# A transformer block on one core: one of the four W2 weight pieces of the second QKV stage is prepared in the last attention unit of the first row

## The chip, the core and the metric

The kernel runs on one NeuronCore of a Trainium2 chip. Five engines of that core appear in this text: PE (TensorE, matrix products; its weight loads are listed apart as PEld), DVE (VectorE), ACT (ScalarE), POOL (GpSimd) and SP (SyncE, which here only issues DMAs; its queue is listed as SPq). The metric is the device time of one execution in microseconds (us).

## What is computed

One transformer block with modulation by a condition, in f32, for x of shape (2, 2048, 512): two batch rows of 2048 tokens. There are 16 heads of 32 columns; the MLP is 2048 wide.

```python
mod = silu(condition) @ Wada + bada
sh_a, sc_a, gt_a, sh_m, sc_m, gt_m = split(mod, 6, axis=1)
xm = layernorm(x, g1, be1) * (1 + sc_a) + sh_a
q, k, v = heads(xm @ Wqkv)
attn = softmax(causal(q @ k.T * 32 ** -0.5))
x = x + gt_a * ((attn @ v) @ Wproj + bproj)
xm = layernorm(x, g2, be2) * (1 + sc_m) + sh_m
x = x + gt_m * (gelu(xm @ W1 + b1) @ W2 + b2)
```

## The kernel before

The two batch rows go through the first half of the block one after the other, each as a `Row` object, and the MLP then takes both at once. The stages, by the trace's time from the start of the span:

- QKV of row 0, to about 167 us: layernorm statistics on DVE, scaling of x on ACT, transposes and products on PE. The products use the Strassen-Winograd form: a 2 x 2 block product with seven multiplications in place of eight, which needs sums of blocks on both sides.
- Attention of row 0 (`attention_phase`, L619), to about 715. Its 16 units are the pairs of a group c of four heads and a block i of 512 queries. The last group takes its query blocks in the order 0, 2, 1, 3, so the last unit is group 3, block 3, with 15 steps. A step is one tile of 128 keys (two where they are cut by the causal edge) for the four heads: PE makes the scores `st`, ACT the exponentials `e` (L670), POOL zeroes what lies behind the diagonal (L682, an affine_select), PE multiplies by the values `vv`, and the exponentials of a unit are summed into a chain `ee` (`add`, L693), which PE then sums over the keys with a matrix of ones (`sm`). The sums of exponentials run on POOL as one operation over four heads; in the last unit alone they run on DVE, as four operations, one a head (L698). Beside that PE and DVE already work out the row maxima of the unit to come (`s`, `mx`).
- Projection of row 0 and the statistics of the second layernorm (`project_phase`, L1295), to about 777.
- QKV of row 1, the second QKV stage, to about 950; attention of row 1, to about 1463; its projection, to about 1525; the MLP of both rows, to the end.

The last unit also prepares the projection behind it (`prepare`, L448): at its steps 5 to 9 DVE copies and multiplies the gate into Wproj (L456, L457, L461), at steps 11 to 14 POOL adds a bias to four tiles of x (L467, tiles named kst because they lie in old key room) and DVE multiplies outputs by reciprocal sums (L469). In the projection POOL adds the bias to the next tiles (L1338) and multiplies later outputs by reciprocals (L1351).

The MLP, too, uses the Strassen-Winograd form, and its weights are put into that form ahead of time, in twelve "pieces" made by the class `Pieces` (L1205): eight of W1 in the first QKV stage (f = 0 to 7) and four of W2 in the second (f = 8 to 11). A W2 piece has seven blocks of 128 x 896 f32, and each block is itself seven sub-blocks of 128 columns. `load` puts eight DMAs of 128 KB into SP's queue (L1239). `add` queues the sums, all on POOL (L1251): four over whole blocks (512 wide) for the outer form, then four for each of the tiles that hold the blocks, over the sub-blocks of the inner form. `store` writes the seven blocks to the scratch array w2d with DMAs that POOL issues (L1271). `plan(f, room, load, start)` says at which tick the piece is loaded and from which its sums are queued; `tick` issues one queued operation, or two where more than 12 are waiting. The blocks lie in room that is not in use just then: spare key and query tiles and the part of the value tile `vv` that row 1 hasn't reached. In the second QKV stage, one tick goes with each step of PE's products:

```python
for f, (room, load, start) in enumerate((
    (room_2, 0, 6), (room_1, 16, 24), (room_2, 47, 56), (room_3, 74, 80),
), FC // 2):
    pieces.plan(f, room, load, start)
```

Each engine takes its instructions in the order in which the program issues them; every DMA of SP and POOL stands in the queue of the engine that issues it, and what waits holds up all behind it. So the order of work around the change follows from where in the program a tick, a load of x (L919) or a `prepare` step stands. PE's order comes from the same program text, with due times for the scores of later units (`due`).

The names to follow are these: kst and qst are key and query tiles (and whatever is kept in their room), vv the values, e the exponentials, ee their sum, x, k, lo the rows and stored keys of the QKV stage, ps_xt the transposes of x.

Of the kernel before, what the change touches and what calls it, by code (L numbers as in the profile page):

```python
# [8 lines left out]
F32 = mybir.dt.float32  # L9
# [8 lines left out]
P = 128  # L18
# [9 lines left out]
def dit_block_kernel(  # L28
# [36 lines left out]
    nc = tc.nc  # L65
# [3 lines left out]
    FC = HID // P  # L69
    NT = T // P  # L70
# [13 lines left out]
    def pool(name, bufs=1, **kw):  # L84
        return tc.tile_pool(name=name, bufs=bufs, reuse_waits="tile", **kw)
# [31 lines left out]
    for n in range(2):  # L117

        f = bp.tile([P, QB + P], BF16, tag=f"fold{n}", name=f"fold{n}")
# [10 lines left out]
    def picks():  # L130
# [61 lines left out]
    w2d = [  # L192
        dram.tile([P, C, 7, P], F32, tag=f"w2d{n}", name=f"w2d{n}")
        for n in range(7)
    ]
# [12 lines left out]
    def act(ins):  # L208

        return tc.keep_in_program_order(ins)  # L210
# [84 lines left out]
    class Row:  # L295


        def __init__(self, b):
            self.b = b
            self.vv = bp.tile([P, NT, D], F32, tag="vv", name="vv")  # L300
            self.kst, self.qst, self.pools = {}, {}, {0: bp}
            self.at = 0
            self.todo = [
                item for u, (_, i) in enumerate(units) for item in self.banks_of(u, i)
            ]
            self.mx = None
            self.unsplit, self.paced = [], False
            self.spent = 0
            self.rows_made = 0

        def banks_of(self, u, i):

            for h in range(HC):
                for t in range(TQ):
                    for kb in range(i):
                        yield u, kb, [(h, t)]
                    if t == 1 and h % 2:
                        yield u, i, [(h - 1, t), (h, t)]
                    elif t == 2:
                        yield u, i, [(h, 0), (h, t)]  # L320
                    elif t == 3:
                        yield u, i, [(h, t)]
# [296 lines left out]
    def attention_phase(row):  # L619
        b, vv, kst, qst = row.b, row.vv, row.kst, row.qst  # L620
        row.paced = True
        with pool(f"att{b}") as ap, pool(
            f"ps_st{b}", bufs=HC, space=PSUM
        ) as ps_stp, pool(f"ps_o{b}", space=PSUM) as ps_op:
            row.pools[1] = ap

            n_bank = [0]

# [71 lines left out]
            def add_to(u, chain, es):  # L700
                add(u, chain, chain, es)
# [44 lines left out]
            def flush(upto):  # L746
                while pending and pending[0][0] <= upto:
                    pending.pop(0)[1]()
# [25 lines left out]
            for u, (c, i) in enumerate(units):  # L774
# [5 lines left out]
                for n_step, tiles in enumerate(steps_of[u]):  # L780
                    last = n_step == steps - 1
                    if n_step == 0:
# [5 lines left out]
                    n = row.count(  # L788
                        due(u, starts[u] + n_step) - QB // 2,
                        u + AHEAD - (n_step < 2 and u > 0),  # L790
                    )
                    if u == 0 and n_step < LAG:

                        n = max(n, HC)
# [9 lines left out]
                    row.inverses(u, n_step)  # L804
                    if u == len(units) - 1:
                        row.prepare(n_step)
                    if make_rows and not last:
                        row.rows(u + 1)
                    flush(now)
# [30 lines left out]
                    if n_step < i * TQ:  # L840
                        k = n_step % TQ
# [36 lines left out]
                    pending.sort(key=lambda p: p[0])  # L878
                    now += 1
            flush(now + LAG)  # L880

    w1_v = W1.rearrange("(c p) f -> p c f", p=P)
    w2_v = W2.rearrange("(c p) f -> p c f", p=P)
# [2 lines left out]
    S1, S2, A11, S4, A12, A22, S3 = range(7)  # L886
# [11 lines left out]
    class Qkv:  # L898
# [239 lines left out]
        def run(self, hp, also, early=()):  # L1138
# [63 lines left out]
                step()  # L1202
            assert not self.loads

    class Pieces:  # L1205


# [17 lines left out]
        def load(self, f, room):  # L1225
            parts = self.blocks(f, room)
            for n, i, k in BASE:
                if f < FC // 2:
                    at = (f + i * FC // 2) * P
                    nc.sync.dma_start(  # L1230
                        parts[n].rearrange("p (k d) -> p k d", d=P),
                        w1_v[:, k * HK : (k + 1) * HK, at : at + P],
                    )
                    continue
                r = f - FC // 2
                for n2, i2 in ((A11, 0), (A21, 1)):
                    at = (2 * i + i2) * P
                    k0 = 2 * k * C + r
                    nc.sync.dma_start(  # L1239
                        parts[n].rearrange("p (k d) -> p k d", d=P)[:, n2 : n2 + 3 : 2],  # L1240
                        w2_v[:, k0 : k0 + C + 1 : C, at : at + P],
                    )

        def add(self, f, room):
            parts = self.blocks(f, room)

            def sum_of(part):
                for n, x, y, op in SUMS:
                    self.ops.append(
                        lambda n=n, x=x, y=y, op=op: act(  # L1250
                            nc.gpsimd.tensor_tensor(part(n), part(x), part(y), op)  # L1251
                        )
                    )

            if f < FC // 2:
                sum_of(lambda n: parts[n])
            else:
                sum_of(lambda n: parts[n][:, A11 * P : (A22 + 1) * P])
                for _, ap in room():
                    sum_of(lambda n, ap=ap: ap[:, :, n * P : (n + 1) * P])  # L1260

            def store():
                for n0, ap in room():
                    cnt = ap.shape[1]
                    if f < FC // 2:
                        dst = w1d[f].rearrange("p n k d -> p n (k d)")[:, n0 : n0 + cnt]
                        nc.gpsimd.dma_start(dst, ap)
                        continue
                    for k in range(cnt):
                        dst = w2d[n0 + k][:, f - FC // 2].rearrange("p k d -> p (k d)")  # L1270
                        nc.gpsimd.dma_start(dst, ap[:, k])  # L1271

            self.ops.append(store)

# [8 lines left out]
        def done(self):  # L1283
            assert not self.events
            while self.ops:
                self.ops.pop(0)()

    def value_rows(row, lo, hi):
        return row.vv[:, lo:hi].rearrange("p n d -> p (n d)")

    def blocks_of(ap, w):
        n = ap.shape[1] // w
        return ap[:, : n * w].rearrange("p (n x) -> p n x", x=w)
# [65 lines left out]
    row = Row(0)  # L1359
    with pool("wada") as wp, pool("qkv0") as qp, pool("hl0") as hp, pool(  # L1360
# [131 lines left out]
        pieces = Pieces()  # L1492
        spare_q = [row.old_queries().rearrange("p h q -> p (h q)") for _ in range(2)]
        spare_k = [row.key_room(q) for q in (2, 3)]
        w1p, w2p = HK * P, 7 * P
# [24 lines left out]
        qkv.run(hp, also, ((0, 0),))  # L1520
        pieces.done()

    attention_phase(row)


    past, row = row, Row(1)
    with pool("qkv1") as qp, pool("ps_qkv1", bufs=6, space=PSUM) as ps_mm:
        qkv = Qkv(row, qp, ps_mm)
        qkv.xts[0] = past.next_s

        def between(n):
            if n == 6:
                qkv.load_w(nc.gpsimd)
            if 9 <= n < 12:
                qkv.weight_sum(nc.vector, n - 9)
            elif n == 13:
                qkv.weight_sum(nc.gpsimd, 3)
            if n >= 12:
                qkv.token_sum(0, (S1, S2, S3, A22)[n - 12])

            if n < MTT:
                qkv.stats(0, n, True)
            if n in (5, 8):
                qkv.norm(0, n // 8)()
            if n == 8:
                qkv.load_x(1)
            if n >= NT - MTT:
                qkv.stats(1, n - (NT - MTT), True)

        project_phase(past, ps_mm, between)  # L1550

        def also(g, n):
            if (g, n) == (0, 10):
                qkv.value_weight_sums()
            pieces.tick()

        with pool("hl1") as hp:
            qkv.load_wv(hp, nc.gpsimd)
            pieces = Pieces()
            spare_q = [row.old_queries().rearrange("p h q -> p (h q)") for _ in range(2)]  # L1560
            spare_k = [row.key_room(q) for q in (2, 3)]

            def room_1():
                return [
                    (0, blocks_of(value_rows(row, 4, 8), w2p)),
                    (2, blocks_of(value_rows(row, 8, NT), w2p)),
                    (6, blocks_of(spare_q[0], w2p)[:, 1:]),
                ]

            def room_3():  # L1570
                return [
                    (0, blocks_of(value_rows(row, 8, NT), w2p)),
                    (4, blocks_of(spare_k[1], w2p)),
                    (6, blocks_of(spare_q[0], w2p)[:, 1:]),
                ]

            for f, (room, load, start) in enumerate((
                (room_2, 0, 6), (room_1, 16, 24), (room_2, 47, 56), (room_3, 74, 80),
            ), FC // 2):
                pieces.plan(f, room, load, start)  # L1580
            qkv.run(hp, also)
            pieces.done()
# [8 lines left out]
    with ExitStack() as mlp:  # L1591
# [74 lines left out]
        w7 = []  # L1666
# [137 lines left out]
        class Hidden:  # L1804
# [99 lines left out]
            def part(self, half, g, f):  # L1904
                return self.h[g][(half * HF + f) // C][:, f % C, :]
# [421 lines left out]
```

## Time and profile before

| | |
|---|---|
| three runs | 2256.35, 2258.96, 2259.01 us; median 2258.96 |
| the profiled execution | 2256.73 us; its span is 2255.0 us |
| PE busy | 2211.3 us, 98% of the span, 12057 instructions |
| PEld busy | 1432.2 us, 64% |
| DVE busy | 1535.7 us, 68%, 3309 instructions |
| POOL busy | 1297.9 us, 58%, 807 instructions |
| ACT busy | 1004.6 us, 45%, 2012 instructions |
| mean granted PE clock | 0.997 |

The span is what the profiler saw between the first instruction and the last. Rows of the trace read like this: start in us, duration in us, engine, source line, operation, output<-inputs by the program's names, shapes, and a count if neighbouring equal instructions are drawn together; in square brackets the idle time of the engine just before the row and what ended it. Groups of instructions read: line, engine, operation, tiles, shapes, count | busy us, mean ns of one | idle us before them. Rows of windows read: from and to, length, then the busy time of each engine with its count of instructions (x), the granted PE clock as a share of full speed, the busy share of the DMA engines and the GB/s they moved.

### The profile page before, as it was taken

What the parts mean: (1) busy time and instruction counts of PE and PEld (TensorE: products, weight loads), DVE (VectorE), ACT (ScalarE), POOL (GpSimd) and SP (SyncE); (2) the same over time, 40 slices, a digit from 0 to 9 for tenths busy, and PEclk for the clock granted to TensorE, in tenths of its full rate; (3) what the DMA queues carried; (4) which work ended last, traced back from release to release, by engine and by line L of the source; (5) the groups of instructions that cost most, each with busy time, mean ns of one, the idle gap of its engine ahead of it and who ended that gap; (6) DMA issues with size and microseconds to landing.
All of it is one profiled execution on the core that took longest, in us unless ns stands there. A gap on an engine that the chain in (4) does not pass through costs nothing.

```text
span 2255.0 us, 33464 instructions
## 1 busy us (share of the span) xinstructions
PE 2211.3 (98%) x12057; PEld 1432.2 (64%) x12057; DVE 1535.7 (68%) x3309; ACT 1004.6 (45%) x2012; POOL 1297.9 (58%) x807
## 2 busy tenths in 40 slices
PE   7999999999999999999999999999999999999998
PEld 6777555555543587855555555345787787688687
DVE  4668766777757666777577767663685586576576
ACT  4434555555564244365656555614322422332410
POOL 4253998998983695199989898444205204304210
PEclk9999999999999999999999999999999999999999
DMA  8877143231324799542324113363353354353433
GB/s 281 251 259 193 43 93 75 62 85 48 106 97 135 252 308 313 142 92 62 85 67 104 44 48 131 109 231 129 109 175 133 123 184 145 108 187 126 158 125 110
DMA packets 160510, 311.57 MB, mean 138 GB/s; under 512 B 16544, under 2 KB 48844, under 8 KB 158552
## 3 DMA queue, kind: packets, MB, share of 16 engines
q1 hardware_dynamic: 155488, 285.53, 41.8%
q0 software_dynamic: 4480, 23.36, 2.7%
q8 instruction: 95, 1.56, 0.3%
q14 instruction: 71, 0.58, 0.1%
q10 hardware_dynamic: 376, 0.55, 0.1%
HBM read 229.95 MB, written 87.29 MB: 141 GB/s over the span
## 4 chain that ended last, share of the span: by engine, by line
PE 89%; DVE 4%; DMA 2%; POOL 2%; ACT 1%; issue 1%; SPq 0%; DVEq 0%; ACTq 0%; POOLq 0%
PE ps_a L206 27%; PE st L206 18%; PE ps_b L206 12%; PE o L206 10%; PE s L206 9%; PE ps_c L206 4%; PE ps_o L206 4%; PE sm L206 3%; DVE junk L498 1%; POOL ee L695 1%; PE ps_xt L214 1%; DMA x<-in_x_dram 1%; ACT e L670 1%; DVE mx L504 1%; PE ps_o L214 1%
## 5 line engine op out<-in xcount | busy, mean ns | idle before, releaser
L670 ACT ACTIVATE e<-st 128x512 f32<-128x512 f32 (+1 forms) x1152 | 575.0, 579 | 362.4 <-PE st L206 321.3
L504 DVE TENSOR_REDUCE mx<-s 128x1 f32<-128x512 f32 x576 | 381.9, 686 | 199.0 <-PE s L206 197.9
L695 POOL TENSOR_TENSOR ee<-ee,e 128x2048 f32<-128x2048 f32 x106 | 485.8, 4583 | 10.3 <-ACT e L670 4.3
L206 PE MATMUL st<-qst,kst 128*128 128x512 f32 (+3 forms) x1280 | 408.7, 386 | 0.0
L206 PE MATMUL s<-kst,qst 128*128 128x512 f32 (+3 forms) x1046 | 382.2, 396 | 8.0 <-DVE mx L498 2.7
L206 PE MATMUL ps_a<-sum,w 128*128 128x256 f32 (+1 forms) x1088 | 328.8, 431 | 0.1
L206 PE MATMUL o<-e,vv 128*32 128x512 f32 (+3 forms) x2560 | 293.2, 537 | 0.3 <-POOL e L682 0.3
L206 PEld LDWEIGHTS st<-qst,kst 128*128 128x128 f32 x1280 | 228.5, 188 | 97.3 <-issue 65.7
L498 DVE CUSTOM_DVE_ANT_0 junk<-s,causal 128x128 bf16<-128x128 f32 (+3 forms) x470 | 220.7, 470 | 61.0 <-PE s L206 46.8
L1795 POOL TENSOR_TENSOR sum<-w 128x256 f32<-128x256 f32 x30 | 21.8, 727 | 397.1 <-DMA w<-w1d 203.1
L206 PEld LDWEIGHTS s<-kst,qst 128*128 128x128 f32 x1046 | 195.4, 189 | 72.4 <-DVE mx L504 15.4
L206 PEld LDWEIGHTS ps_a<-sum,w 128*128 128x128 f32 x1088 | 204.5, 190 | 40.1 <-issue 11.4
L695 POOL TENSOR_TENSOR ee<-e 128x2048 f32<-128x2048 f32 x42 | 192.5, 4583 | 43.5 <-ACT e L670 42.5
L206 PEld LDWEIGHTS <-sel 32*128 32x128 bf16 x1152 | 29.5, 91 | 197.0 <-issue 196.1
L2014 ACT ACTIVATE h<-h,cols 128x512 f32<-128x512 f32 x120 | 76.8, 710 | 136.3 <-DVE h L1716 136.3
L504 DVE TENSOR_REDUCE mx<-st 128x1 f32<-128x512 f32 x192 | 131.0, 682 | 0.5
L682 POOL TENSOR_SCALAR_AFFINE_SELECT e<-e 128x512 f32<-128x512 f32 x128 | 83.3, 669 | 67.2 <-ACT e L670 67.2
L206 PE MATMUL st<-fold,sel 32*128 32x512 bf16 (+1 forms) x1152 | 117.3, 372 | 1.2
L206 PEld LDWEIGHTS o<-e,vv 128*32 128x32 f32 x2560 | 59.1, 108 | 92.3 <-issue 72.8
L1716 DVE TENSOR_TENSOR h<-c,ps_b 128x256 f32<-128x256 f32 x90 | 37.9, 421 | 103.5 <-PE ps_b L206 103.0
L1066 POOL TENSOR_TENSOR lo<-lo,hi 128x512 fp32r<-128x512 f32 x32 | 40.7, 1274 | 114.2 <-ACT hi L1064 109.8
L206 PE MATMUL ps_b<-sum,w 128*128 128x256 f32 (+1 forms) x384 | 95.0, 383 | 0.0
(237 smaller groups left out, 3590.7 us busy)
## 6 DMA issues: line engine op xcount, KB each, us to landing
qst<-q SPq DMA_DIRECT2D x128, 256.0 KB
kst<-k SPq DMA_DIRECT2D x128, 256.0 KB
w<-w1d SPq DMA_DIRECT2D x32, 896.0 KB
w<-w2d SPq DMA_DIRECT2D x28, 1024.0 KB
w<-w2d SPq DMA_DIRECT2D x28, 768.0 KB
q<-hi SPq DMA_DIRECT2D x32, 256.0 KB
q<-lo SPq DMA_DIRECT2D x32, 256.0 KB
k<-hi SPq DMA_DIRECT2D x32, 256.0 KB
```

The costliest lines, as they stand in the source:

```text
L206: return tc.keep_in_program_order(nc.tensor.matmul(*args, **kw))
L214: return tc.keep_in_program_order(nc.tensor.transpose(dst, src, ident[:n, :n]))
L498: nc.vector.tensor_tensor_reduce(junk[:, :w], x, causal[:, QB - w :], 1.0, MASKED, ALU.add, ALU.max, m,)
L504: self.vector(nc.vector.tensor_reduce(m, x, axis=AX.X, op=ALU.max))
L670: act(nc.scalar.activation(e4[:, h, :w], sts[h][:, :w], AF.Exp))
L682: nc.gpsimd.affine_select(d, d, pattern=[[0, HC], [1, P]], compare_op=ALU.is_ge, fill=0.0, base=0, channel_multiplier=-1,)
L695: act(nc.gpsimd.tensor_tensor(dst, x, y, ALU.add))
L1066: engine.tensor_tensor(lo, d, hi.bitcast(F32), ALU.subtract)
L1716: act(nc.vector.tensor_tensor(dst, x, y, ALU.add))
L1795: act(engine.tensor_tensor(dst, u, v, op))
L2014: nc.scalar.activation(d[j], d[j], AF.Gelu, bias=col(r_b1 + half * HF + fs[j], 1))
```

## The change

The first of the four W2 pieces, f = FC // 2 = 8, leaves the second QKV stage and is made in the last attention unit of row 0. The other three keep the rooms and ticks that the first three plans had, so f = 9, 10 and 11 now stand at (0, 6), (16, 24) and (47, 56); the plan with `room_3` is gone.

In the last unit of row 0 each step makes two ticks. The piece is loaded at tick 3 and its sums are queued from tick 10, which is step 5; what is left is issued after the unit's last operation. Its seven blocks lie in the first 384 columns of `vv`, tiles 0 to 6 (three blocks) and 7 to 13 (three blocks), values of head groups 0 to 2 that no later unit reads, and in a new tile `w7` of the attention pool (one block). A block in `vv` is seven runs of 128 columns, with 512 bytes each, in every partition, where the old room had one run of 896 columns.

The diff, where lines of context are cut:

```diff
@@ class Row
+            self.in_last_unit = self.finish_pieces = None
@@ attention_phase
-            row.pools[1] = ap
+            row.pools[1] = row.spare_pool = ap
...
                     if u == len(units) - 1:
                         row.prepare(n_step)
+                        if row.in_last_unit:
+                            row.in_last_unit()
...
             flush(now + LAG)
+            if row.finish_pieces:
+                row.finish_pieces()
@@ class Pieces
+    def split_up(ap):
+        return ap.rearrange("p (k d) -> p k d", d=P) if len(ap.shape) == 2 else ap
...
-                        parts[n].rearrange("p (k d) -> p k d", d=P)[:, n2 : n2 + 3 : 2],
+                        split_up(parts[n])[:, n2 : n2 + 3 : 2],
...
-                sum_of(lambda n: parts[n][:, A11 * P : (A22 + 1) * P])
+                sum_of(lambda n: split_up(parts[n])[:, A11 : A22 + 1])
                 for _, ap in room():
-                    sum_of(lambda n, ap=ap: ap[:, :, n * P : (n + 1) * P])
+                    if len(ap.shape) == 3:
+                        sum_of(lambda n, ap=ap: ap[:, :, n * P : (n + 1) * P])
+                    else:
+                        sum_of(lambda n, ap=ap: ap[:, :, n])
...
-                        dst = w2d[n0 + k][:, f - FC // 2].rearrange("p k d -> p (k d)")
-                        nc.gpsimd.dma_start(dst, ap[:, k])
+                        nc.gpsimd.dma_start(
+                            w2d[n0 + k][:, f - FC // 2], split_up(ap[:, k])
+                        )
...
+    def pieces_in_dead_values(row, f):
+        pieces = Pieces()
+
+        def room(extra=[]):
+            if not extra:
+                t = row.spare_pool.tile([P, 1, 7 * P], F32, tag="w7", name="w7p")
+                extra.append(t)
+            dead = [
+                row.vv[:, t : t + 7, : 3 * P].rearrange("p t (n d) -> p n t d", d=P)
+                for t in (0, 7)
+            ]
+            whole = extra[0].rearrange("p n (t d) -> p n t d", d=P)
+            return [(0, dead[0]), (3, dead[1]), (6, whole)]
+
+        pieces.plan(f, room, 3, 10)
+
+        def step():
+            for _ in range(2):
+                pieces.tick()
+
+        row.finish_pieces = pieces.done
+        return step
...
+    row.in_last_unit = pieces_in_dead_values(row, FC // 2)
     attention_phase(row)
@@ second QKV stage
-            def room_3():
-                return [
-                    (0, blocks_of(value_rows(row, 8, NT), w2p)),
-                    (4, blocks_of(spare_k[1], w2p)),
-                    (6, blocks_of(spare_q[0], w2p)[:, 1:]),
-                ]
-
             for f, (room, load, start) in enumerate((
-                (room_2, 0, 6), (room_1, 16, 24), (room_2, 47, 56), (room_3, 74, 80),
-            ), FC // 2):
+                (room_2, 0, 6), (room_1, 16, 24), (room_2, 47, 56),
+            ), FC // 2 + 1):
                 pieces.plan(f, room, load, start)
```

## The prediction

> **What bounds the kernel now.** I read the page's span first, then busy time by stage, then the gaps of PE in the two stages that the change touches, and there SP, POOL and DVE.
>
> ```profile
> span 2255.0 us, 33464 instructions
> ```
>
> ```profile
> core 0: us, PE busy (x) PEld busy (x) DVE busy (x) ACT busy (x) POOL busy (x), PEclk, DMA share, GB/s
> 167.00:715.00 548.00, 541.95 (x3675) 290.48 (x3673) 398.02 (x963) 317.46 (x636) 447.49 (x176) 1.00 0.34 92
> 715.00:777.00 62.00, 60.69 (x160) 28.56 (x160) 40.55 (x78) 13.43 (x25) 35.35 (x29) 1.00 0.72 238
> 777.00:950.00 173.00, 167.11 (x796) 145.34 (x795) 115.53 (x268) 71.53 (x161) 106.66 (x124) 0.99 0.78 254
> ```
>
> These are attention of row 0, its projection and the second QKV stage. PE is busy nearly all the time, so a stage is worth its PE gaps and no more: 173.00 - 167.11 = 5.9 us in the QKV stage. The largest gap there, and how PE ran behind it:
>
> ```profile
> 876.68 0.33 PE L214 MATMUL ps_xt<-ident,x 128*128 128x128 f32 x1 [3.79 <-ACT x L964]
> 877.38 1.75 PE L214 MATMUL ps_xt<-ident,x 128*128 128x128 f32 x7 [0.38 <-ACT x L964]
> ...
> 890.42 1.04 PE L214 MATMUL ps_xt<-ident,x 128*128 128x128 f32 x8
> ```
>
> ```profile
> 876.00:878.00 2.00, 0.95 (x4) 0.76 (x5) 0.00 (x0) 2.00 (x3) 2.00 (x2) 0.72 1.00 206
> 878.00:880.00 2.00, 2.00 (x9) 1.81 (x8) 0.40 (x1) 1.72 (x5) 1.92 (x3) 0.50 0.89 200
> 880.00:882.00 2.00, 2.00 (x10) 1.71 (x10) 1.34 (x4) 1.56 (x3) 2.00 (x4) 0.93 1.07 219
> ```
>
> PE waited 3.79 + 0.38 us for rows of x scaled on ACT. It then ran at a granted clock of 0.50: seven transposes took 1.75 us, where eight take 1.04 later. Why x is late stands in SP's queue:
>
> ```profile
> 860.83 0.32 SPq L1031 DMA_DIRECT2D k<-lo  x1
> 861.25 0.93 SPq L1239 DMA_DIRECT2D vv<-in_L_cond_W_dram  x2
> ...
> 864.33 0.93 SPq L1239 DMA_DIRECT2D kst<-in_L_cond_W_dram  x2
> 865.36 1.84 SPq L919 DMA_DIRECT2D x<-in_x_dram  x4
> ```
>
> The eight loads of the fourth W2 piece (four rows of two, the first and last shown) stand between k<-lo and the four loads of x and hold x up by 865.36 - 861.25 = 4.11 us.
>
> Where the piece goes, the last attention unit of row 0, POOL has two holes, 672.3 to 686.5 and 688.2 to 705.4:
>
> ```profile
> 671.64 0.63 POOL L682 TENSOR_SCALAR_AFFINE_SELECT e<-e 128x512 f32<-128x512 f32 x1
> 686.53 1.66 POOL L467 TENSOR_TENSOR kst<-kst,bgate 128x512 f32<-128x512 f32 x1 [14.25 <-DVE bgate L457]
> 705.36 1.44 POOL L682 TENSOR_SCALAR_AFFINE_SELECT e<-e 128x512 f32<-128x512 f32 x1 [17.17 <-ACT e L670]
> 706.77 1.27 POOL L467 TENSOR_TENSOR kst<-kst,bgate 128x512 f32<-128x512 f32 x1
> 708.00 2.13 POOL L682 TENSOR_SCALAR_AFFINE_SELECT e<-e 128x512 f32<-128x512 f32 x2
> 710.10 1.69 POOL L467 TENSOR_TENSOR kst<-kst,bgate 128x512 f32<-128x512 f32 x1
> 711.75 1.08 POOL L682 TENSOR_SCALAR_AFFINE_SELECT e<-e 128x512 f32<-128x512 f32 x1
> ...
> 714.48 4.93 POOL L1351 TENSOR_TENSOR kst<-kst,qst 128x512 f32<-128x512 f32 x4
> ```
>
> DVE, which here adds the exponentials itself, has next to none:
>
> ```profile
> 672.36 2.50 DVE L698 TENSOR_TENSOR ee<-e 128x512 f32<-128x512 f32 x4 [6.01 <-ACT e L670]
> 676.02 4.94 DVE L698 TENSOR_TENSOR ee<-ee,e 128x512 f32<-128x512 f32 x8 [1.17 <-ACT e L670]
> 685.03 0.69 DVE L456 COPY qst<-ps_rows 128x512 f32<-128x512 f32 x1 [4.07 <-PE ps_rows L206]
> ...
> 686.37 3.58 DVE L698 TENSOR_TENSOR ee<-e 128x512 f32<-128x512 f32 x4
> ...
> 699.60 2.49 DVE L698 TENSOR_TENSOR ee<-ee,e 128x512 f32<-128x512 f32 x4
> ...
> 705.02 1.28 DVE L469 TENSOR_TENSOR kst<-kst,qst 128x512 f32<-128x512 f32 x2
> 706.83 5.51 DVE L698 TENSOR_TENSOR ee<-ee,e 128x512 f32<-128x512 f32 x4 [0.53 <-POOL e L682]
> ```
>
> ```profile
> 712.39 0.62 PE L206 MATMUL sm<-ee,ones 128*32 128x512 f32 x1 [0.63 <-DVE ee L698]
> ```
>
> Two readings carry the forecast. From 685.03 to 706.3 no DVE row has an idle time in brackets, and PE's row sums of the last chain wait for its last add: what makes DVE late after 685 makes the end of the unit late. And the two engines disturb each other. Four adds take 2.49 us while POOL is silent, 3.58 when they meet the one POOL sum at 686.53, and 5.51 among POOL's operations after 705.36. There the engines take turns: from 708.00 to 711.75 POOL does two selects and a sum, 0.60 + 0.60 + 1.23 us by themselves (0.63 alone less 0.03 of overlap; 4.93 / 4), in 3.75 us, so it pays (3.75 - 2.43) / 3 = 0.44 us for the add that each lets in, and DVE gets one add per POOL operation.
>
> The Trainium skill, SBUF — State Buffer, section "SBUF: two separate sides", calls this an exclusive lock held for the whole instruction, against VectorE instructions with two SBUF inputs. By whole adds of 0.60 a turn would be 0.16 dearer than the rows' 0.44, and the end some 2 us later still; the sum keeps 0.44.
>
> **The change part by part.** *Taken out of the QKV stage:* 8 loads on SP, 20 sums and 7 stores on POOL (the list of the changed kernel's instructions shows this and three pieces left, the x loads now right behind k<-lo). x is issued 4.11 us sooner, against a gap of 3.79 + 0.38 = 4.17, and DVE's statistics of x no longer meet POOL's sums. The half clock goes with the gap: seven transposes cost 0.84 us more than at 1.04 / 8 each, and the slow stretch holds other matmuls too; by the granted clocks of the three stretches of 2 us, the stretch at half speed lasts (1 - 0.72) x 2 / 0.5 + 2 + (1 - 0.93) x 2 / 0.5 = 3.4 us, in which 1.7 is lost. Gain: 4.17 + 1.7 = 5.9. Bounds: 0, if k<-lo and the wait for PE then hold x as long, and 5.9 + 1.4 for the stage's other gap at most. I take 5.9, since nothing else stands ahead of x.
>
> *Loads, now in row 0:* the list puts all eight ahead of the load of Wproj, long before 672; the DMA share of that stage is 0.34. Two wait for PE's last use of old value columns ahead of the last unit's queries. The later of them needs the value product that the first row below shows, over at 591.4, before those queries go out:
>
> ```profile
> 590.35 1.06 PE L206 MATMUL o<-e,vv 128*32 128x512 f32 x8
> ```
>
> ```profile
> 592.80 1.75 SPq L360 DMA_DIRECT2D qst<-q  x4
> ```
>
> So they cost nothing; without that cover the queries would go out later by the difference.
>
> *Sums and stores, now in the last unit.* POOL's list is: 4 sums of 512 and 7 of 384, one store, one of 384 and three of 128, five stores, the first L467 sum (once at 686.53), one of 128, the last store; then the old order from the select at 705.36 on. Prices:
>
> ```profile
> L1251 POOL TENSOR_TENSOR vv<-vv 128x512 f32<-128x512 f32 x5 | 6.2, 1266 | 0.2
> L1251 POOL TENSOR_TENSOR kst<-kst 128x256 f32<-128x256 f32 x4 | 2.8, 731 | 0.0
> L1271 POOL DMA_DIRECT2D w2d<-vv x4 | 2.2, 554 | 0.0
> L1251 POOL TENSOR_TENSOR qst<-qst 128x128 f32<-128x128 f32 x4 | 1.7, 461 | 0.0
> ```
>
> ```profile
> 741.61 2.96 POOL L926 DMA_DIRECT2D wqk<-in_L_cond_Wqkv_dram  x4
> ```
>
> Start to start these are 1.23, 0.69 and 0.42 us; 384 lies between, 0.95. A store of one run per partition takes 0.55 and a load of two runs 2.96 / 4 = 0.74; the six new stores from vv have seven runs, so 0.55 to 0.55 + 6 x 0.19 = 1.7, and 3.9 if every run cost a whole store. I take 1.7: about 10 us for all seven, in which DVE is free. Work without waits: 16 us of sums and 10 of stores, in 31 us of holes.
>
> With turns: (1) from 672.27 eleven sums meet the twelve adds of 672.36 and 676.02: 4 x (1.23 + 0.44) + 7 x (0.95 + 0.44) = 16.4, so the adds end at 689.0, not 680.96. The 4.07 us idle before 685.03 take up half: copy and gate (1.34) end at 690.3, not 686.37, 3.9 late. (2) The next four adds meet one 384 and three 128, 0.95 + 3 x 0.42 + 4 x 0.44 = 4.0, against 3.58 before: 4.3 late. (3) The L467 sum that they met before is met later, with one of 128: 1.23 + 0.42 more, 5.9 late. No idle time is left to take it up. (4) So at 706.5, when the selects begin (a little late, with PE), DVE has some 12 operations to the last add, and POOL 11: 4 selects, 3 L467 sums and the 4 of L1351, which until now ran after DVE had finished. In turns 4 x 0.60 + 7 x 1.23 + 11 x 0.44 = 15.9, and 0.6 for the twelfth: 723.0, against 706.83 + 5.51 = 712.34. The unit ends 10.6 us late, nearly all of it as a PE gap of over 5 us and smaller ones before the last adds. After 3.79 us of gap the clock halved, so I add 1.7. The projection behind is PE work with 62.00 - 60.69 = 1.3 us of gaps and gives nothing back. Bounds: 0, if the adds never meet the sums, and 15, if turns are dearer and the slow clock lasts twice as long.
>
> The Trainium skill, TensorE: Matmul & The Clock Gate, section "What's actually happening", puts the half clock behind one idle window of 3.4 us that runs free of the kernel; a gap of 5.5 us need not hold a whole one, so by that rule the 1.7 may be 0 here. The trace shows one slow stretch behind one gap of 3.79.
>
> Sum: 10.6 + 1.7 - 5.9 = +6.4. The profiled run took 2256.73 (its span and 1.73 around it), which gives 2263.1; the three runs have their median 2.2 above it, and 2258.96 + 6.4 = 2265.
>
> **The rivals.** *Late, but not into the tail:* DVE is 4 to 6 us behind at 700, yet POOL's L1351 sums find it done, because ACT and PE hold the selects back meanwhile. For it: PE's later sums slow ACT too. Against: nothing in rows after 705.36 gates L1351 but POOL itself. +4 - 5.9 = -2: 2257. *Hidden:* POOL gives way to the adds and works in DVE's idle time, 31 us of holes for 26 of work. For it: the size. Against: 5.51 against 2.49. -5.9: 2253, faster. *No gain in QKV:* the x loads, sooner, still land late at a DMA share of 0.97 (0.78 over the stage), or another wait follows at once. Then 10.6 + 1.7 = +12.3: 2271. From 5.9 us of net delay in the last unit on, the change loses; that is the point which decides between the signs. *It does not do what it says:* the stores may be so dear (3.9 each) that POOL reaches the select of 705.36 some 8 us late; then PE waits for the select instead, and the L1351 sums come after the adds: about +8 in that unit, +2 in all, 2261.
>
> **How the numbers follow.** Forecast 0.52, late but not into the tail 0.17, hidden 0.14, no gain in QKV 0.12, dear stores 0.05. What a measurement of this kernel can tell from no change is about 0.2%, 4.5 us. Hidden is faster, with 0.03 of the second: 0.17. The rest of the second, the stores and small sums of the forecast (0.03) are within: 0.22. Slower: 0.61. Range 2254 to 2271: it leaves out the end of hidden and the worst of no gain; the forecast's own range is 2260 to 2270.
>
> **What would show it.** In the changed kernel L698 rows between 672 and 694 should have about 1.4 to 1.7 us an add; DVE should lack its 4 us of idle time before the copy of ps_rows; PE should wait for DVE ee at the unit's end, 5 us or more in one row; the projection should start near 726, not 715.1; behind it a granted clock of 0.50. In QKV the wait for x at ps_xt should fall below 0.5. It is wrong if adds keep 0.62 us beside POOL, or if the gap of 3.79 stays.

## The result, and the profile after

The changed kernel takes 2260.95 us (median of 17 runs, 2256.58 to 2266.24), the kernel before 2257.51 us in the runs beside it (median of 17, 2254.0 to 2260.75). The ratio is 1.0018 with a 95% interval of 1.0011 to 1.0024, about 4.1 us more (the two medians alone differ by 3.4): slower, clear of zero, but just under the 0.2% that the prediction set as its measure. Single runs of either kernel scatter by several us, so stages are compared below within profiled executions, by how much later the same instruction starts in the one trace than in the other.

The profiled execution of the changed kernel took 2262.91 us, with a span of 2261.2. The last unit ends with the copy of its attention output:

```profile
723.42 0.58 ACT L734 COPY ot<-o 128x512 f32<-128x512 f32 x1 [8.13 <-PE o L206]
```

Its windows from there on:

```profile
core 0: us, PE busy (x) PEld busy (x) DVE busy (x) ACT busy (x) POOL busy (x), PEclk, DMA share, GB/s
723.65:787.00 63.35, 60.72 (x160) 28.58 (x160) 41.27 (x78) 13.46 (x25) 35.41 (x29) 1.00 0.74 231
777.00:950.00 173.00, 168.71 (x793) 143.78 (x792) 117.67 (x272) 71.49 (x162) 92.33 (x103) 1.00 0.75 241
```

Before, the same copy started at 714.77:

```profile
714.77 0.58 ACT L733 COPY ot<-o 128x512 f32<-128x512 f32 x1 [5.49 <-PE o L206]
```

Four instructions of ACT give the whole account. Source lines have moved down by one to some forty lines in the changed kernel.

| instruction of ACT | start before | start after | later by | the stage's share |
|---|---|---|---|---|
| exponentials at the start of the last unit | 668.28 | 668.97 | 0.69 | scatter of the first stage |
| output copy of the last unit | 714.77 | 723.42 | 8.65 | last unit +7.96 |
| hi<-lo in the first products of QKV | 778.97 | 788.94 | 9.97 | projection +1.32 |
| a late vv<-ps_a of QKV | 944.68 | 950.44 | 5.76 | second QKV stage -4.21 |
| end of the span | 2255.0 | 2261.2 | 6.2 | the rest +0.4 |

So the last unit loses 8 us, the QKV stage gives 4 back, and the rest is small. In the last unit DVE's adds are the place. First its rows in time, then its groups of adds over the unit, of after and of before:

```profile
673.06 6.82 DVE L699 TENSOR_TENSOR ee<-e 128x512 f32<-128x512 f32 x4 [5.63 <-ACT e L671]
679.80 12.36 DVE L699 TENSOR_TENSOR ee<-ee,e 128x512 f32<-128x512 f32 x8
692.08 0.68 DVE L457 COPY qst<-ps_rows 128x512 f32<-128x512 f32 x1
...
715.48 5.51 DVE L699 TENSOR_TENSOR ee<-ee,e 128x512 f32<-128x512 f32 x4 [0.53 <-POOL e L683]
```

```profile
L699 DVE TENSOR_TENSOR ee<-ee,e 128x512 f32<-128x512 f32 x28 | 29.2, 1102 | 0.5 <-POOL e L683 0.5
L699 DVE TENSOR_TENSOR ee<-e 128x512 f32<-128x512 f32 x12 | 13.1, 1153 | 5.6 <-ACT e L671 5.6
```

```profile
L698 DVE TENSOR_TENSOR ee<-ee,e 128x512 f32<-128x512 f32 x28 | 20.4, 789 | 1.7 <-ACT e L670 1.2 <-POOL e L682 0.5
L698 DVE TENSOR_TENSOR ee<-e 128x512 f32<-128x512 f32 x12 | 8.6, 774 | 6.0 <-ACT e L670 6.0
...
L456 DVE COPY qst<-ps_rows 128x512 f32<-128x512 f32 x1 | 0.7, 692 | 4.1 <-PE ps_rows L206 4.1
```

The forty adds took 42.3 us in place of 29.0, 13.3 more. Of that 1.2 and 4.1 us went into idle time that DVE had before, ahead of the eight adds from 676.02 and ahead of the copy; 13.3 - 5.3 = 8.0 is left. The last four adds start at 715.48 in place of 706.83, 8.65 later: with the 0.69 of the start taken off, 7.96, the delay of the whole unit. POOL's rows show what the adds met:

```profile
672.94 1.30 POOL L1259 TENSOR_TENSOR vv<-vv 128x512 f32<-128x512 f32 x1
674.17 1.76 POOL L1259 TENSOR_TENSOR w7p<-vv 128x512 f32<-128x512 f32 x1
675.88 13.34 POOL L1259 TENSOR_TENSOR vv<-vv 128x512 f32<-128x512 f32 x9
689.16 1.00 POOL L1281 DMA_DIRECT2D w2d<-vv  x1
690.18 1.01 POOL L1259 TENSOR_TENSOR vv<-vv 128x384 f32<-128x384 f32 x1
691.13 1.74 POOL L1259 TENSOR_TENSOR w7p<-w7p 128x128 f32<-128x128 f32 x3
692.83 4.70 POOL L1281 DMA_DIRECT2D w2d<-vv  x5
...
711.38 4.06 POOL L683 TENSOR_SCALAR_AFFINE_SELECT e<-e 128x512 f32<-128x512 f32 x1 [10.56 <-DVE kst L470]
...
723.11 4.94 POOL L1387 TENSOR_TENSOR kst<-kst,qst 128x512 f32<-128x512 f32 x4
```

Eleven sums stand beside eleven of the first twelve adds, one to one; the stores follow; and the select at 711.38, which took 1.44 before, took 4.06. PE's waits in the unit and in the scores of the QKV stage, and the transposes of x that were late before:

```profile
692.81 0.40 PE L206 MATMUL st<-fold,sel 32*128 32x512 bf16 x4 [3.67 <-DVE qst L457]
715.50 1.07 PE L206 MATMUL o<-e,vv 128*32 128x512 f32 x8 [1.10 <-POOL e L683]
717.78 1.93 PE L206 MATMUL o<-e,vv 128*32 128x384 f32 x16 [1.22 <-POOL e L683]
...
879.51 0.50 PE L206 MATMUL s<-kst,qst 128*128 128x512 f32 x1 [0.71 <-DVE mx L505]
881.10 0.50 PE L206 MATMUL s<-kst,qst 128*128 128x512 f32 x1 [0.23 <-DVE mx L505]
...
884.49 1.04 PE L214 MATMUL ps_xt<-ident,x 128*128 128x128 f32 x8
```

The gap of 3.79 us that stood at the transposes is gone, and eight of them take 1.04 us, at full clock. Two new waits of 0.71 and 0.23 us stand shortly before.

### The profile page after: what moved, and what is told of

Read it like the earlier page. It is cut to its first block, busy times and chain, and to the rows that moved or that the text cites. A ratio compares the mean times of both kernels' runs of the same rounds, so it can differ in the third digit from the quotient of the medians.

```text
span 2261.2 us, 33477 instructions
## 1 busy us (share of the span) xinstructions
PE 2213.6 (98%) x12057; PEld 1432.0 (63%) x12057; DVE 1549.1 (69%) x3309; ACT 1003.3 (44%) x2012; POOL 1309.6 (58%) x807
## 4 chain that ended last, share of the span: by engine, by line
PE 88%; DVE 4%; DMA 2%; POOL 2%; issue 1%; ACT 1%; SPq 0%; DVEq 0%; ACTq 0%; POOLq 0%
PE ps_a L206 27%; PE st L206 18%; PE ps_b L206 12%; PE o L206 10%; PE s L206 9%; PE ps_c L206 4%; PE sm L206 3%; PE ps_o L206 2%; POOL ee L696 1%; DVE junk L499 1%; PE ps_xt L214 1%; ACT e L671 1%; DVE mx L505 1%; PE ps_o L214 1%; DVE stat L218 0%
```

## The experiments

All were run beside the kernel before. For each, the delay of the last unit (from the exponentials at its start to its output copy) and of the QKV stage was taken from its own trace against the trace of before, as in the table above.

| kernel | ratio to before, 95% interval | last unit | QKV stage | forty adds of the unit |
|---|---|---|---|---|
| changed kernel | 1.0018, 1.0011 to 1.0024 | +8.0 | -4.2 | 42.3 us |
| no_piece | 0.9982, 0.9973 to 0.9992 | 0.0 | -5.0 | 29.0 |
| x_first | 0.9982, 0.9973 to 0.9991 | 0.0 | -3.8 | 29.0 |
| no_stores | 1.0000, 0.9991 to 1.0009 | +5.9 | -2.8 | 40.2 |
| small_sums | 0.9985, 0.9975 to 0.9995 | +0.3 | -4.9 | 30.6 |
| gate_act | 1.0007, 0.9998 to 1.0017 | +8.1 | -4.2 | 42.5 |
| no_sums | 1.0012, 1.0003 to 1.0021 | 0.0 | -5.0 | 29.0 |

The six kernels with three pieces in the QKV stage gain 2.8 to 5.0 us there. That spread is not explained, and each value is from one execution, so differences of about 1 us in that column carry no argument.

**no_piece: the piece left out of the last unit.** From the changed kernel:

```diff
-    row.in_last_unit = pieces_in_dead_values(row, FC // 2)
...
+                    if row.b == 0 and n_step == 1 and 4 <= u < 11:
+                        nc.sync.dma_start(w2d[u - 4][:, 0], w2_v[:, :7, :P])
```

> The changed kernel without the piece in the last unit (its place in the scratch array is filled by seven plain copies of W2 blocks, issued by SP in units 4 to 10 of row 0, so the output is not the reference's). Theory (the last unit and the projection lose, the QKV stage gains): the last unit ends where it ended before (within 0.5 us of 712.3 for the last add), and the stage from 777 on keeps the changed kernel's gain of 4.2 us; time 4 to 6 us below the kernel before, ratio about 0.9975 to 0.998. Rival (the loss of the changed kernel isn't in the unit but in what follows, such as the first QKV products or the clock): 0 to +3 us.

The median was 2253.19 us, ratio 0.9982. The unit is not late at all, and the QKV stage keeps its gain. So the 8 us of the last unit are all due to the piece's work there, and a gain of about 4 us is what taking the fourth piece out of the QKV stage brings here by itself.

**x_first: the kernel before, with x ahead of the piece's loads.**

```diff
                         if n == 3 and g + 1 not in self.xts:
                             self.load_x(g + 1)
+                        if row.b and (g, n) == (1, 32):
+                            self.load_x(g + 2)
```

> The kernel before, with the four loads of x for the last token group of the second QKV stage issued ahead of the fourth piece's eight loads; all four pieces stay. Theory (the gap came from the x loads' place in SP's queue): PE's gap of 3.79 us at ps_xt falls below 0.5 and no half clock follows; 4 to 6 us faster than before, ratio about 0.9975 to 0.998. Rival (the gap closed in the changed kernel because 20 sums and 7 stores of POOL left, so that DVE's statistics and POOL's splits come sooner): a gap of 2 us or more remains somewhere in the stage, and the time is within 1.5 us of before.

The median was 2252.65 us, ratio 0.9982: as much as without the fourth piece, with all four pieces in place. SP's queue and the transposes:

```profile
856.94 0.32 SPq L1031 DMA_DIRECT2D k<-lo  x1
857.35 1.82 SPq L919 DMA_DIRECT2D x<-in_x_dram  x4
859.28 0.90 SPq L1241 DMA_DIRECT2D vv<-in_L_cond_W_dram  x2
```

```profile
865.34 0.50 PE L206 MATMUL s<-kst,qst 128*128 128x512 f32 x1 [0.72 <-DVE mx L504]
866.93 0.50 PE L206 MATMUL s<-kst,qst 128*128 128x512 f32 x1 [0.23 <-DVE mx L504]
...
870.31 1.04 PE L214 MATMUL ps_xt<-ident,x 128*128 128x128 f32 x8
```

x is issued right behind k<-lo, the transposes wait for nothing, and the same two new waits for DVE's maxima appear, with 20 more sums on POOL than in the changed kernel. The rival, that the gap closed because POOL had less to do, is out. So the place of eight loads in one queue accounts for 3.8 us where the changed kernel gained 4.2, a difference inside the spread above, and no work has to be moved for it.

**no_sums: a miss.** From the changed kernel:

```diff
                 for n, x, y, op in SUMS:
+                    if f == FC // 2:
+                        continue
...
                 for n0, ap in room():
+                    if f == FC // 2 and n0 == 6:
+                        ap = room()[1][1][:, 2:3]
```

> The changed kernel with the piece's 20 sums left out; its loads and seven stores stay in the last unit (output not the reference's). Theory (turns between sums and adds cost the unit its 8 us): the twelve adds from 672.4 take 0.62 us each again, the copy of ps_rows comes within 1 us of 685.0 in the time of before, and the last unit ends less than 1.5 us late; time 3 to 5 us below before. Rival (POOL's DMA issues hold DVE out, 0.94 us each): the unit still ends 4 us or more late and the time is within 2 us of before.

With no sums to wait for, the stores did not stay in the last unit: in the built program they were moved forward to wherever their blocks were ready. The first two were issued in the first stage, and the rest before the last unit:

```profile
102.16 1.92 POOL L1285 DMA_DIRECT2D w2d<-vv  x2 [39.48 <-DVE mhl L526]
```

So the run says nothing on stores beside adds. Its unit was on time, with 29.0 us of adds, because neither sums nor stores were there. Its ratio is above 1, although its profiled execution, the fastest of its ten, lost nothing in these stages. In the first stage PE waited 5.37 us for DVE's maxima (the row at 122.63), where the same row before waited 2.75; that goes the right way, but what the slower executions lost was not traced and stays open.

**no_stores: the sums alone.**

```diff
-            self.ops.append(store)
+            if f != FC // 2:
+                self.ops.append(store)
...
+                    if row.b == 0 and n_step == 1 and 4 <= u < 11:
+                        nc.sync.dma_start(w2d[u - 4][:, 0], w2_v[:, :7, :P])
```

> The changed kernel with the piece's seven stores left out and its loads and 20 sums kept (plain copies of W2 blocks fill their place, issued by SP in units 4 to 10; output not the reference's). Theory (sums cost most): copy of ps_rows some 4 to 5 us late, last add 5 to 7 us late, time within 2 us of before. Rival (the stores hold DVE out and are most of it): last add less than 3 us late, time 3 to 5 us below before.

The median was 2257.16 us, ratio 1.0000. The unit is 5.9 us late. Its adds:

```profile
L699 DVE TENSOR_TENSOR ee<-ee,e 128x512 f32<-128x512 f32 x28 | 26.8, 1020 | 0.5 <-POOL e L683 0.5
L699 DVE TENSOR_TENSOR ee<-e 128x512 f32<-128x512 f32 x12 | 13.4, 1177 | 6.0 <-ACT e L671 6.0
```

They take 40.2 us, 11.2 more than before; less the same 5.3 of idle time that is 5.9, the delay found. So the sums are 5.9 of the 8.0, and by difference the stores among them the other 2.1. The copy of ps_rows starts here at

```profile
687.66 0.68 DVE L457 COPY qst<-ps_rows 128x512 f32<-128x512 f32 x1
```

in a unit that began 2.8 us earlier than before: 5.4 us late, against 6.4 in the changed kernel. So about half of the stores' 2.1 us was lost ahead of the copy.

**small_sums: the sums made short, so that the stores stay where they are.**

```diff
-                            nc.gpsimd.tensor_tensor(part(n), part(x), part(y), op)
+                            nc.gpsimd.tensor_tensor(
+                                *(
+                                    part(m) if f != FC // 2 or n in whole
+                                    else part(m)[..., :8]
+                                    for m in (n, x, y)
+                                ),
+                                op,
+                            )
```

Here `whole` names the five sums into w7.

> The changed kernel with 15 of the piece's 20 sums cut to 8 columns of each sub-block (those into the tile w7 keep their width), so that the seven stores stay in their place behind them; output not the reference's. Theory (the time that POOL's sums hold DVE out is what costs): the twelve adds from 672.4 lose some 4 us or less in place of 12, the copy of ps_rows comes less than 2 us late, the last add less than 3 us late; ratio to before 0.9980 to 0.9993. Rival (each operation of POOL, however short, and each store costs an add its turn): the last add still 5 us or more late, ratio above 1.0003.

The median was 2253.12 us, ratio 0.9985. POOL and DVE in the first part of the unit:

```profile
669.80 1.74 POOL L1259 TENSOR_TENSOR w7p<-vv 128x512 f32<-128x512 f32 x1
671.50 5.23 POOL L1259 TENSOR_TENSOR vv<-vv 128x32 f32<-128x32 f32 x8
676.68 1.00 POOL L1289 DMA_DIRECT2D w2d<-vv  x1
...
680.37 3.76 POOL L1289 DMA_DIRECT2D w2d<-vv  x4
```

```profile
669.70 3.71 DVE L699 TENSOR_TENSOR ee<-e 128x512 f32<-128x512 f32 x4 [6.65 <-ACT e L671]
673.37 5.19 DVE L699 TENSOR_TENSOR ee<-ee,e 128x512 f32<-128x512 f32 x8
682.40 0.69 DVE L457 COPY qst<-ps_rows 128x512 f32<-128x512 f32 x1 [3.84 <-PE ps_rows L206]
```

As many POOL operations as in the changed kernel cost the adds 1.6 us in all (30.6 against 29.0), most of it in the first four, beside the sum into w7 that kept its width; the eight adds behind them took 5.19 us, where alone they took 4.94. What costs is the time that POOL's sums last, not their number. Of the stores it shows less: of the four from 680.37 on, two fell into DVE's idle time ahead of the copy. The two before them, at 676.68 and 677.96, ran beside adds that kept 0.72 us each, so a store does not always hold an add up.

**gate_act: the copy that PE waited for taken off DVE.**

```diff
-                act(nc.vector.tensor_copy(self.gate, ps))
+                act(nc.scalar.copy(self.gate, ps))
```

> The changed kernel with the copy of ps_rows to the gate done on ACT, not on DVE (both rows). Theory (the backlog of adds on DVE sets the end of the unit): PE's wait of 3.67 us for that copy goes, but PE waits about as long for tiles that the late adds or the late select hold; the last add comes at most 1.5 us earlier in the unit than in the changed kernel (8.0 us late there); ratio to before 1.0008 to 1.0022. Rival (the PSUM bank that waits for the copy is the loss, 5.3 us of the 8): the unit ends 4 to 6 us earlier than in the changed kernel; ratio 0.9985 to 1.0000.

The median was 2258.42 us, ratio 1.0007, just below the range that was expected; the interval overlaps with the changed kernel's, so the times alone do not decide, and the trace has to. PE no longer waits 3.67 us at 692.81. It waits here:

```profile
690.45 0.62 PE L206 MATMUL sm<-ee,ones 128*32 128x512 f32 x1 [0.62 <-DVE ee L699]
696.04 0.86 PE L206 MATMUL st<-fold,sel 32*128 32x512 bf16 x2 [0.93 <-ACT e L671]
713.53 1.94 PE L206 MATMUL o<-e,vv 128*32 128x512 f32 x8 [2.41 <-POOL e L683]
715.81 1.94 PE L206 MATMUL o<-e,vv 128*32 128x384 f32 x16 [0.34 <-POOL e L683]
```

```profile
708.60 4.88 POOL L683 TENSOR_SCALAR_AFFINE_SELECT e<-e 128x512 f32<-128x512 f32 x1 [9.14 <-ACT e L671]
```

The unit ends 8.1 us late, as in the changed kernel. ACT now waits for DVE's adds (2.68 us ahead of its exponentials at 690.49, 2.84 ahead of those at 695.39), and PE comes earlier to the end and finds the adds and the select as late as ever. The longest wait in the trace was not the cause; removing it moved it.

x_first, whose output is complete, is faster than the kernel before, and so than the changed one: 0.18% below the kernel before (interval 0.09% to 0.27%).

## Why the prediction held, and where not

The mechanism held: DVE's adds and POOL's sums take turns in the last unit, the lateness exceeds what the QKV stage gives back, and the kernel gets slower. The forecast of +6.4 us was too high by some 2 us (measured 4.1, interval 2.5 to 5.4); 2260.95 lies inside the forecast's own range of 2260 to 2270, near its lower end. Step by step:

- **Sums against the first twelve adds (1).** The price of a turn was right: six starts from 679.80 to the seventh of the eight adds take 1.41 us each, 0.95 for a sum of 384 and 0.46 for the turn, where 0.44 was forecast; the eleven sums took 16.2 us, forecast 16.4. The twelfth add was not. It was to take 0.6 and took 2.47, ending at 692.15:

```profile
688.27 3.88 DVE L699 TENSOR_TENSOR ee<-ee,e 128x512 f32<-128x512 f32 x2
```

  The first of these two ends at 689.76, by the other adds' 1.49. The second waited through a store, a sum of 384 and one of 128. The term that failed is "about 10 us for all seven, in which DVE is free": DVE was not free throughout (the add at 694.00, beside two later stores, took 1.77 us as well). The seven took less than forecast, 1.00 + 4.70 + 0.58 = 6.3 us, but their cost to DVE was put at nothing. The copy came 6.4 us late (7.05 less the start's 0.69), not 3.9. Without any store it still came 5.4 late (no_stores), since the twelfth add then meets the twelfth sum; no_stores puts the stores' share of the unit's delay at 2.1.
- **The next adds, and the late L468 sum (2, 3).** Forecast +0.4 and +1.6, measured +0.3 and +1.4. At the multiplication that started at 692.98 before and at 701.62 after, DVE was 8.0 us late (the start's 0.69 taken off), forecast 5.9, and it kept that lateness to the end.
- **The last adds beside the L1351 sums (4).** This was the largest error: 4.7 us more forecast, none found. The step put POOL's eleven operations beside DVE's last twelve from 706.5 on. But the first select was not "a little late": it began 6.0 us later than before (711.38 against 705.36), as ACT's exponentials came later by as much behind PE's wait of 3.67 us for the copy and its slow stretch; and it got no turn while DVE worked through its backlog (711.38 to 715.44). So POOL was as late as DVE, the last four adds met the same four operations as before and took 5.51 us again, and the multiplications of L1351 (now L1387) began at 723.11, after the last add at 720.99. The rival "late, but not into the tail" had this part right: ACT and PE did hold the select back. But in gate_act they held it less, it began at 708.60, and it still ended only behind DVE's row of adds; so the backlog decides, and that was 8 us, not the rival's 4 to 6.
- **The half clock (+1.7).** The clock halved twice, as these windows show, but inside the unit, while PE was ahead of DVE and would have waited anyway: gate_act had no slow stretch behind the copy, ran at 0.66 on average from 711 to 721, and its unit ended as late. The projection ran at 1.00 from 723.65.

```profile
692.00:694.00 2.00, 1.19 (x7) 0.80 (x7) 1.97 (x4) 0.27 (x1) 2.00 (x4) 0.86 0.14 41
694.00:696.00 2.00, 2.00 (x11) 0.65 (x13) 2.00 (x3) 1.80 (x4) 2.00 (x3) 0.50 0.80 229
696.00:698.00 2.00, 2.00 (x16) 0.30 (x8) 2.00 (x5) 0.00 (x0) 1.98 (x3) 0.79 0.88 252
...
716.00:718.00 2.00, 0.78 (x12) 0.20 (x8) 2.00 (x2) 0.00 (x0) 2.00 (x3) 0.83 0.84 283
718.00:720.00 2.00, 2.00 (x19) 0.75 (x14) 2.00 (x3) 0.00 (x0) 2.00 (x2) 0.50 0.99 399
720.00:722.00 2.00, 2.00 (x24) 0.57 (x22) 2.00 (x2) 0.00 (x0) 2.00 (x3) 0.82 0.55 229
```

  The projection did lose 1.3 us, but at two waits, 1.16 us for POOL's products and 1.43 for a split on ACT. In the traces whose unit ended on time the first was 0.20 to 0.86 us and the second 0.67 to 1.33, and in gate_act, as late as the changed kernel, 0.47 and 0.95; so that loss is not shown to come from the change.
- **The QKV gain (-5.9).** The gap and its half clock went, as forecast: PE's own instructions were 10.28 us late at 868 of before, 11.76 at 872 and 5.78 from 881 on, so 6.0 us were won. But 1.5 had been lost just ahead, 0.94 of it at the new waits for DVE's maxima, and 0.3 earlier: -4.2 in the stage. "Nothing else stands ahead of x" was right for SP's queue, and left out who else waits for DVE once the statistics of x come sooner. That these statistics delay the maxima is read from the rows, not tried.
- **Loads.** They cost nothing, as forecast: from the first stage to the last unit the two traces differ by less than 0.3 us.

The profile's markers: adds of 1.4 to 1.7 us (1.71 and 1.55), no idle time before the copy, and no wait at ps_xt came as stated. The wait of 5 us or more for ee at the unit's end did not: PE waited for the copy and the selects. Nor did the half clock behind the unit, or a projection start near 726 (it was 723.74).

The four parts in one line: forecast 5.9 + 4.7 + 1.7 - 5.9 = +6.4; found in the profile 8.0 + 0 + 1.3 - 4.2 = +5.1, and over all runs +4.1. That the sums lie so near each other is in part luck: against the forecast the parts were off by +2.1, -4.7, -0.4 (1.7 forecast for the half clock, 1.3 found at two waits in its place) and +1.7, and most of that cancelled.

## What to carry to other kernels

Idle time of one engine is no free room when the engine beside it is full and the two shut each other out: count what the work does to the neighbour (here 13.3 us more of adds for 20 sums and 7 stores), subtract the neighbour's idle time, and the rest is the delay. Ask first what in the old place made the work dear; here it was the position of eight loads in a queue, and moving four other loads ahead of them won as much time over all runs as taking the work away did. And remove the longest wait before blaming it: where another engine is late behind it, the wait only moves.

## What the runs showed of the hardware

- **A select of POOL gets no turn in a row of DVE adds, a sum does.** Selects that began while DVE worked through such a row took 1.44 us before (one more DVE operation began meanwhile), 3.05 in no_stores (four), 4.06 in the changed kernel (five) and 4.88 in gate_act (seven), and ended about 0.5 us after DVE's row did. A sum of POOL that began in the same way (686.53 in the trace of before) took 1.66 and was let in after one add. Once POOL was at work, selects too alternated with adds. The Trainium skill, SBUF — State Buffer, section "SBUF: two separate sides", lets the operation that starts first keep the ports for its whole length; that sums and adds alternated one to one agrees with that, though beside a sum an add cost 0.46 us, less than its 0.60 alone; the select's wait over five DVE operations shows that a waiting operation need not be the next.
- **POOL's issue of a store can hold DVE out.** The last of the first twelve adds, from 689.69 on, waited through one of 1.00 us and the two sums behind it; later adds beside stores waited in part or not at all, and in small_sums two stores ran beside adds without any loss. What decides is not shown.
- **A store of seven runs per partition costs POOL 0.94 us** (4.70 / 5), against 0.55 for one run.
- **Half clock behind short gaps.** The second slow stretch, from about 717 on, came behind two waits of 1.10 and 1.22 us with products between them, not one long one. Each slow stretch lost 1.7 us by its granted clocks, as the one in the QKV stage of before. Nor does a wait's length decide alone: at one wait for DVE's maxima in the first stage, 2.75 us before and 2.82 in no_stores, the granted clock from 120 to 128 was 0.63 before and 1.00 in no_stores. The prediction counted one slow stretch before; this is another, and single executions differ with it: no_stores, x_first, small_sums and gate_act, at full clock there, reached the last unit 1.1 to 3.5 us sooner than before.
